# Both exponentials of a unit's first step placed ahead of the next unit's copies of logits in ScalarE's order

## The chip, the cores and the metric

The kernel runs on one core of a Trainium2 chip. The core has a matrix engine (TensorE, PE in the profile), a vector engine (VectorE, DVE), an activation engine (ScalarE, ACT), GpSimd (POOL) and SyncE (SP), which here only issues DMAs. Each engine works through its own instructions in the order in which the program lists them, and waits at an instruction until the semaphores that it names have come. The metric is the device time of one execution in microseconds (us); less is better. Before the change it is 3184.22 us, the median of three runs (3184.0 to 3186.14).

## What is computed

Eight images of 512 channels and 32 x 32 pixels pass two layers in float32. The first layer normalizes over groups, and applies a block with two bottlenecks, each of which holds a 3 x 3 convolution and an attention over all 1024 pixels with 4 heads of 64 channels; the second normalizes again and applies a grouped 1 x 1 convolution whose groups come from tables. What matters here is the attention:

```python
qkv = conv2d(x, qkv_w, 0).reshape(b, 3, HEADS, HD, hw)
q, k, v = (qkv[:, 0], qkv[:, 1], qkv[:, 2])
r = (rw + rh).reshape(1, HEADS, HD, hw)
logits = jnp.einsum('bhdi,bhdj->bhij', q, k + r) * HD ** (-0.5)
a = jax.nn.softmax(logits, axis=-1)
out = jnp.einsum('bhij,bhdj->bhdi', a, v)
...
z = jax.nn.silu(bn_eval(conv2d(z, m_cv2_w[i], 0), m_cv2_bn[i]))
ys.append(yi + z)
```

Around it stand `t = cbs(x, cv1_w, ...)`, `z = cbs(yi, m_cv1_w[i], ..., 1)` and `cbs(concatenate(ys), cv2_w, ...)`, where `cbs` is a convolution, a scale and shift per channel, and SiLU.

## The kernel before

**Units.** The attention is cut into 64 units, counted here from 0. A unit is one image, one of the two bottlenecks, one pair of heads (`hp`) and one half of the queries (512 of them). Its keys come in 8 chunks `t` of 128 (`KT = 8`). The logits of a chunk are held with the keys on the partitions and 512 queries of each of the two heads along the row, as a tile `st` of 128 x 1024 in SBUF.

**What a unit issues** (class `Unit`):

- `logits(t)`: TensorE multiplies a chunk of keys with the queries into two PSUM banks `lg`, one for each head (L511); ScalarE copies each bank to `st` (L518); from the second chunk on VectorE takes the running maximum `mx` over the chunks (L523), reading the bank as well.
- `top()` and `spread()`: TensorE transposes `mx`, VectorE reduces it to the negated maximum of each query (`nm`, L532), and TensorE spreads that over the partitions (`mb`, L540).
- `soften(t)`: VectorE adds `mb` to `st` (L545). `exponent(t)`: ScalarE takes the exponential of `st` in place (L549), and from the second chunk on GpSimd adds it to the sum `acc` in four pieces (L556).
- `values(t)`: TensorE multiplies the exponentials with `v` and accumulates over all eight chunks in one bank `po` (L563). There is one such bank for all units (`ps_o`, one buffer).
- `finish()`: TensorE sums `acc` over the partitions into a bank `den` (L577), and ScalarE copies that to `rb` (L580). `divide(part)`: VectorE takes the reciprocal of `rb` (L584) and multiplies `po` with it into `q` (L586), a half at a time. Only then may the next unit's first `values` write `po`.

**The loop.** Units overlap: while unit `u` takes exponentials and multiplies with `v`, the logits of the next unit `nxt` are computed. A unit has four steps, `t` = 0, 2, 4 and 6, with two chunks each. In the first step the unit before it (`before`) is also brought to its end: its `finish`, its last two `values` and its `divide`.

**Background work.** All other matrix work (the 1 x 1 and 3 x 3 convolutions, `q`, `k`, `v`, and so on) is kept in generators. After each step `advance` takes as much of it as a share of a counted time says, so that TensorE has work between a step's chain of softmax operations and the next. `clock.tick` moves the counted time on, and operations that are set for a due time (the normalization of loaded tiles, L165, for one) are issued when it has passed. Background results are read by ScalarE as SiLU (L130) or copies, and by VectorE.

**Banks.** `lg`, `den`, the transposed maxima and all background results share five PSUM banks (`ps_f`). The ten `st` buffers (`stp`) hold the eight chunks of a unit and the first two of the next.

**What sets the order.** A scheduler places the instructions of each engine before the program runs. Where its choice isn't wanted the order is written out by hand: `pe_turn`, `act_turn` and `in_turn` tie each instruction that is passed to them to the one passed before it on the same engine (TensorE, ScalarE, VectorE). For ScalarE only two kinds are tied so: the copies of logits, and the exponentials:

```python
act_turn(nc.scalar.copy(st[:, h], lg[h]))        # logits, L518
act_turn(nc.scalar.activation(st, st, AF.Exp))   # exponent, L549
```

The copy of `den` to `rb`, the SiLUs, the normalizations and the other copies are not tied. ScalarE loads a table (ACT_TABLE_LOAD in the profile) when it goes from SiLU to the exponential, and again when it goes back; plain copies need none.

In steps 2, 4 and 6 ScalarE's tied order is `exponent(t)`, four copies, `exponent(t + 1)`. In step 0 it is four copies, `exponent(0)`, `exponent(1)`.

Of the kernel before, what the change touches and what calls it, by code (L numbers as in the profile page):

```python
# [39 lines left out]
def conv_preact_kernel(ctx: ExitStack, tc: tile.TileContext, x, cv1, cv2, mcv1, qkv, mcv2, bn, rw, rh, conv, s_in, t_in, out):  # L40
# [868 lines left out]
    def slot_filler(s):  # L909

        prev = slots[s - 1] if s else (None, 0)
        nxt = slots[s + 1] if s + 1 < len(slots) else (None, 0)
        todo, needed = [], 0.0

        def add(us, g):
            nonlocal needed
            todo.append((us, g))
            needed += us

        im, i = nxt  # L920
        add(8.0, bg.take(8.0))
        if im and i == 1:
            add(7.0, im.conv_m2(0))
            add(0.0, call(im.transform, 1, 3.0, 1.0))
            add(9.0, bg.take(9.0))
        products = im.conv3(i) if im else iter(())
        if prev[1] == 1:
            if im:
                add(21.3, (us for _, us in zip(range(16), products)))
            add(7.0, prev[0].conv_m2(1))  # L930
            add(0.0, call(lambda: finishing(prev[0])))
        if im:
            add(10.7 if prev[1] == 1 else 32.0, products)
            add(7.0, bg.take(7.0))
        if im:
            add(21.0, im.project(i))
        if s + 2 < len(slots) and slots[s + 2][1] == 0:
            add(0.0, call(slots[s + 2][0].load_y))
            add(0.0, call(slots[s + 2][0].transform, 0, 8.0, 1.3))
        rest = SHARE - needed if im else 70.0  # L940
        if rest > 0:
            todo.append((rest, bg.take(rest, wait=True)))
        total = sum(c for c, _ in todo)
        return needed, total, todo
# [77 lines left out]
    for s in range(len(slots)):  # L1022
        needed, total, todo = slot_filler(s)
        state = {"done": 0.0}

        def filler():
            for us, g in todo:
                start = state["done"]
                for cost in g:
                    clock.tick(cost)  # L1030
                    state["done"] += cost
                    yield

                state["done"] = max(state["done"], start + us)

        fill = filler()

        def advance(share):
            goal = max(share * total, min(1.0, share / 0.74) * needed + 0.1)
            while state["done"] < goal:  # L1040
                if next(fill, "end") == "end":
                    break

        steps = 4 * (KT + 2)
        for j in range(4):
            u = units[4 * s + j]
            nxt = units[4 * s + j + 1] if 4 * s + j + 1 < len(units) else None
            base = j * (KT + 2)

            advance((base + 0.7) / steps)  # L1050
            u.top()
            clock.tick(0.9)
            advance((base + 1.4) / steps)
            u.spread()
            clock.tick(0.9)
            advance((base + 2) / steps)
            for t in range(0, KT, 2):
                if before and t == 0:
                    before.finish()
                    clock.tick(0.9)  # L1060
                u.soften(t)
                u.soften(t + 1)
                if t:
                    u.exponent(t)

                lag = u if t else before
                if lag:
                    lag.values((t - 2) % KT)
                    lag.values((t - 1) % KT)
                    clock.tick(2.0)  # L1070
                if before and t == 0:
                    before.divide(0)
                    before.divide(1)
                if nxt:
                    nxt.logits(t)
                    nxt.logits(t + 1)
                    clock.tick(2.0)

                if not t:
                    u.exponent(t)  # L1080
                u.exponent(t + 1)
                advance((base + 4 + t) / steps)
            before = u
        for _ in fill:
            pass
# [62 lines left out]
```

## Time and profile before

| | |
|---|---|
| time of three runs, median (lowest to highest) | 3184.22 us (3184.0 to 3186.14) |
| the profiled execution's own time | 3188.51 us |
| its span, first to last instruction | 3186.8 us |
| mean granted clock of TensorE | 0.993 |
| busy: TensorE matmuls / VectorE / ScalarE / GpSimd | 3085.9 / 2050.6 / 1717.3 / 1395.3 us |
| 512 exponentials (L549) | 539.1 us, 1068 ns each |
| 1024 copies of logits (L518) | 524.4 us, 596 ns each |
| 2048 matmul records of `values` (L563) | 500.3 us; TensorE idle just before them 21.7 us |

The profile is of one execution. A group's row gives its busy time, the mean of one instruction, and the time for which its engine stood idle just before it, with what ended that idle time. A float32 matmul shows as two records, and the two heads' matmuls of `logits`, `values` and `finish` run side by side, so their records overlap. Matmul ends are modelled, and successive ones overlap; what counts is the time from start to start. In a timeline the columns are start, length, engine, line, operation, what is written and read, and, in brackets, the idle time of the engine before it with its releaser. "PEclk" is the granted clock of TensorE as a share of full speed.

### The profile page before, as it was taken

Reading aid. Unit: us, or ns where it says so; the run is one execution under the profiler, and the core shown is the slowest. Engines: PE = TensorE matmul, PEld = TensorE weight load, DVE = VectorE, ACT = ScalarE, POOL = GpSimd, SP = SyncE. Lnnn points to the kernel's source line nnn. Section 1 sums busy time; section 2 is a strip of 40 time slices with the busy share of each in tenths; the row PEclk is TensorE's granted clock in tenths of the full one; section 3 lists DMA queues with packets and bytes.
Section 4 is the critical chain, followed back from the end, with each engine's and each line's share of the span. In section 5 each row is a group of like instructions: output and inputs, shape, how many; then the busy total and the mean of one; then the engine's idle time right before and its main releaser. Section 6 shows DMA issues by size and latency. Waiting matters only on the chain.

```text
span 3186.8 us, 34171 instructions
## 1 busy us (share of the span) xinstructions
PE 3085.9 (97%) x11668; PEld 1522.9 (48%) x11668; DVE 2050.6 (64%) x2718; ACT 1717.3 (54%) x2347; POOL 1395.3 (44%) x1867
## 2 busy tenths in 40 slices
PE   7999999999999999999999999999999999999999
PEld 3645444454445454454445454454445454453333
DVE  5446576667666676667666676667766676666742
ACT  3255765854655555544656455554656455555631
POOL 2114444446444454445444454355434454455420
PEclk9999999999999999999999999999999999999999
DMA  8851442421233232424233332424233332413366
GB/s 294 287 187 63 154 161 83 149 79 65 88 109 129 93 119 70 148 86 137 89 109 129 119 114 75 139 83 142 90 113 132 110 122 71 145 63 129 110 212 216
DMA packets 142014, 399.35 MB, mean 125 GB/s; under 512 B 13072, under 2 KB 14352, under 8 KB 141840
## 3 DMA queue, kind: packets, MB, share of 16 engines
q1 hardware_dynamic: 141120, 396.94, 36.4%
q8 instruction: 92, 1.51, 0.2%
q14 instruction: 82, 0.67, 0.1%
q10 hardware_dynamic: 720, 0.23, 0.0%
HBM read 317.42 MB, written 79.69 MB: 125 GB/s over the span
## 4 chain that ended last, share of the span: by engine, by line
PE 70%; DVE 7%; ACT 5%; issue 3%; DMA 2%; POOL 1%; ACTq 0%; DVEq 0%; SPq 0%; POOLq 0%
PE m L313 14%; PE cv L175 12%; PE lg L511 11%; PE po L563 11%; PE qk L175 6%; PE l L175 6%; PE v L405 3%; PE m L175 2%; DVE st L545 2%; PE mb L540 2%; ACT st L518 2%; PE mt L531 2%; PE den L577 2%; DVE mx L523 1%; ACT st L549 1%
## 5 line engine op out<-in xcount | busy, mean ns | idle before, releaser
L556 POOL TENSOR_TENSOR sum<-sum,st 128x256 f32<-128x256 f32 x1536 | 1126.1, 767 | 570.1 <-ACT st L549 565.0
L523 DVE TENSOR_TENSOR mx<-mx,lg 128x512 f32<-128x512 f32 x768 | 477.8, 681 | 412.2 <-ACT st L518 412.2
L549 ACT ACTIVATE st<-st 128x1024 f32<-128x1024 f32 x512 | 539.1, 1068 | 340.2 <-DVE st L545 338.8
L518 ACT COPY st<-lg 128x512 f32<-128x512 f32 x1024 | 524.4, 596 | 351.7 <-PE lg L511 306.6
L545 DVE TENSOR_TENSOR st<-st,mb 128x1024 f32<-128x1024 f32 x512 | 603.7, 1213 | 63.6 <-PE mb L540 63.6
L313 PE MATMUL m<-plane,w_m 128*128 128x256 f32 x2304 | 537.4, 388 | 21.8 <-DVE x2r L487 9.0
L556 POOL TENSOR_TENSOR sum<-st,st 128x256 f32<-128x256 f32 x256 | 188.0, 766 | 789.4 <-ACT st L549 789.3
L563 PE MATMUL po<-st,v 128*64 128x512 f32 x2048 | 500.3, 608 | 21.7 <-ACT st L549 14.7
L511 PE MATMUL lg<-q,k 64*128 64x512 f32 x2048 | 513.7, 619 | 1.6 <-ACT y L130 1.5
L313 PEld LDWEIGHTS m<-plane,w_m 128*128 128x128 f32 x2304 | 433.0, 192 | 149.0 <-issue 44.1
L175 PE MATMUL cv<-y,w_cv 128*128 128x512 f32 x1024 | 465.4, 599 | 10.8 <-DVE mx L523 6.2
L511 PEld LDWEIGHTS lg<-q,k 64*128 64x128 f32 x2048 | 178.6, 187 | 330.1 <-issue 266.4
L175 PEld LDWEIGHTS cv<-y,w_cv 128*128 128x128 f32 x1024 | 185.7, 190 | 251.7 <-issue 227.8
L563 PEld LDWEIGHTS po<-st,v 128*64 128x64 f32 x2048 | 128.9, 137 | 327.5 <-issue 228.9
L175 PE MATMUL l<-x,w_l 128*128 128x512 f32 x512 | 235.8, 603 | 10.3 <-DVE mx L523 10.0
L175 PE MATMUL cv<-x,w_cv 128*128 128x512 f32 x512 | 233.4, 603 | 8.5 <-ACT x L165 2.4
L175 PE MATMUL qk<-z,w_qkv 128*128 128x512 f32 x512 | 234.0, 600 | 1.7 <-DVE mx L523 1.7
L584 DVE RECIPROCAL rb<-rb 128x256 f32<-128x256 f32 x128 | 215.4, 1723 | 30.6 <-ACT rb L580 30.5
L532 DVE TENSOR_REDUCE nm<-mt 128x4 f32<-128x512 f32 x128 | 82.4, 685 | 158.6 <-PE mt L531 158.5
L580 ACT COPY rb<-den 128x512 f32<-128x512 f32 x64 | 37.3, 583 | 226.9 <-PE den L577 226.9
L175 PEld LDWEIGHTS l<-x,w_l 128*128 128x128 f32 x512 | 92.7, 190 | 132.3 <-issue 107.2
L175 PEld LDWEIGHTS cv<-x,w_cv 128*128 128x128 f32 x512 | 94.3, 192 | 126.4 <-issue 107.3
(145 smaller groups left out, 2404.3 us busy)
## 6 DMA issues: line engine op xcount, KB each, us to landing
w_m<-w_m SPq DMA_DIRECT2D x96, 768.0 KB, 4.8
w_cv<-in_cv SPq DMA_DIRECT2D x90, 512.0 KB, 3.5
y<-y SPq DMA_DIRECT2D x64, 512.0 KB, 4.4
x<-in_x SPq DMA_DIRECT2D x56, 512.0 KB, 5.4
y<-y SPq DMA_DIRECT2D x64, 256.0 KB, 3.5
k<-r SPq DMA_DIRECT2D x32, 512.0 KB, 3.6
res<-y SPq DMA_DIRECT2D x32, 512.0 KB, 4.0
xr<-in_x SPq DMA_DIRECT2D x32, 512.0 KB, 4.0
```

The source lines that it names most:

```text
L175: nc.tensor.matmul(ps, w, moving, start=(n == 0), stop=(n == len(terms) - 1))
L313: nc.tensor.matmul(ps[:, ts(co, 256)].rearrange("p (t x) -> p t x", x=F), w[:, co, c, dx], u[:, 9 * c : 9 * c + 8, dx : dx + F], start=(j ...
L405: nc.tensor.matmul(ps[:, ts(j, P)], z[:, c, ts(4 * j4 + j, P)], w[:, c, 512 + P * hp : 512 + P * hp + P], start=(c == 0), stop=(c == IT - 1),)
L511: nc.tensor.matmul(lg[h], self.k[r, ts(t, P)], self.q[r, self.hp, ts(self.half, HALF)], start=True, stop=True)
L518: act_turn(nc.scalar.copy(st[:, h], lg[h]))
L523: in_turn(nc.vector.tensor_tensor(self.mx[:, h], so_far[:, h], lg[h], ALU.max))
L532: nc.vector.tensor_reduce(self.nm[:, h], mt, AX.X, ALU.max, negate=True)
L545: in_turn(nc.vector.tensor_tensor(st, st, flat(self.mb), ALU.add))
L549: act_turn(nc.scalar.activation(st, st, AF.Exp))
L556: nc.gpsimd.tensor_tensor(flat(self.acc)[:, part], flat(so_far)[:, part], st[:, part], ALU.add)
L563: nc.tensor.matmul(self.po[HD * h : HD * h + HD], self.v[:, t, ts(h, HD)], self.st[t][:, h], start=(t == 0), stop=(t == KT - 1),)
L584: nc.vector.reciprocal(self.rb[:, r], self.rb[:, r])
```

## The change

In step 0 both exponentials now stand right after the two `soften`, as in the other steps the first of the two does; so they come ahead of `before.values`, `before.divide` and `nxt.logits` in the program, and ahead of the four copies of logits in ScalarE's tied order. Steps 2, 4 and 6 are as they were. No instruction is added or removed, and no tile or DMA is changed; the counted time of the background work is ticked as before. `exponent(0)` issues one exponential; `exponent(1)` issues one exponential and GpSimd's first four additions to `acc`, which move with it.

```diff
                 u.soften(t)
                 u.soften(t + 1)
-                if t:
-                    u.exponent(t)
+                u.exponent(t)
+                if not t:
+
+                    u.exponent(1)
 
                 lag = u if t else before
                 if lag:
...
                     nxt.logits(t + 1)
                     clock.tick(2.0)
 
-                if not t:
-                    u.exponent(t)
-                u.exponent(t + 1)
+                if t:
+                    u.exponent(t + 1)
                 advance((base + 4 + t) / steps)
```

## The prediction

> **What bounds the kernel now.** First the page: TensorE's busy time, and the chain that ended last.
>
> ```profile
> span 3186.8 us, 34171 instructions
> ...
> PE 3085.9 (97%) x11668; PEld 1522.9 (48%) x11668; DVE 2050.6 (64%) x2718; ACT 1717.3 (54%) x2347; POOL 1395.3 (44%) x1867
> ...
> PE 70%; DVE 7%; ACT 5%; issue 3%; DMA 2%; POOL 1%; ACTq 0%; DVEq 0%; SPq 0%; POOLq 0%
> ```
>
> TensorE works or is about to for 97% of the span; only some 100 us of idle time can be won. The groups of instructions say how much of it the exponentials own:
>
> ```profile
> L563 PE MATMUL po<-st,v 128*64 128x512 f32 x2048 | 500.3, 608 | 21.7 <-ACT st L549 14.7 <-DVE mx L523 6.9
> ```
>
> TensorE stands idle 21.7 us in all before `values`. Next the timelines of step 0. ScalarE in unit 30, which loads a table:
>
> ```profile
> 1557.83 0.58 ACT L580 COPY rb<-den 128x512 f32<-128x512 f32 x1 [5.45 <-PE den L577]
> 1560.64 2.05 ACT L518 COPY st<-lg 128x512 f32<-128x512 f32 x4 [2.23 <-PE lg L511]
> 1562.71 1.28 ACT L549 ACT_TABLE_LOAD   x1
> 1564.00 2.00 ACT L549 ACTIVATE st<-st 128x1024 f32<-128x1024 f32 x2
> ```
>
> ScalarE idles 2.23 us after `rb`, waiting for logits, though the softened tiles lie ready; 2.2 us appears in almost every unit, because `den`, two `values` and two `logits` always take TensorE that long. 37 of the 64 units have the load before `exponent(0)`, 27 don't. Unit 27 is one that does not, and TensorE waits in it (PE, ACT and DVE timelines):
>
> ```profile
> 1441.07 2.02 PE L563 MATMUL po<-st,v 128*64 128x512 f32 x8 [1.23 <-DVE mx L523]
> ...
> 1435.22 0.58 ACT L580 COPY rb<-den 128x512 f32<-128x512 f32 x1 [4.79 <-PE den L577]
> 1438.01 2.05 ACT L518 COPY st<-lg 128x512 f32<-128x512 f32 x4 [2.20 <-PE lg L511]
> 1439.92 2.04 ACT L549 ACTIVATE st<-st 128x1024 f32<-128x1024 f32 x2
> ...
> 1434.25 2.35 DVE L545 TENSOR_TENSOR st<-st,mb 128x1024 f32<-128x1024 f32 x2 [0.95 <-PE mb L540]
> 1436.52 3.36 DVE L584 RECIPROCAL rb<-rb 128x256 f32<-128x256 f32 x2
> 1439.79 0.69 DVE L586 TENSOR_TENSOR q<-po,rb 128x256 f32<-128x256 f32 x2
> ```
>
> The named releaser is doubtful: `values(0)` starts 0.05 us after `exponent(0)` ends (1439.92 + about 1.1), so that is what it waited for. But the last reader of `po`, the multiply of `divide`, ends at 1440.48, 0.59 us before. That is the next wait behind the one removed.
>
> Last, the stretches around unit 60, whose stall is the longest (3.72 us by the PE timeline):
>
> ```profile
> 2916.74:2920.15 3.41, 2.48 (x6) 0.73 (x8) 2.35 (x3) 2.77 (x3) 1.51 (x3) 0.50 0.00 0
> 2920.15:2923.57 3.42, 3.42 (x10) 1.18 (x8) 0.00 (x0) 0.11 (x1) 3.42 (x6) 0.50 0.00 0
> ```
>
> The granted clock (third from the end) is 0.50 in two stretches of 3.4 us after it.
>
> [...]
>
> **The change part by part.** No instruction is added; ScalarE's order in step 0 becomes `rb`, (load), two exponentials, four copies.
>
> *The exponentials, earlier.* Without a load they take 0.96 + 1.06 = 2.0 us and fit the 2.2 us of idle time: the copies do not move. With a load, 0.58 + 1.29 + 2.0 = 3.9 us from the start of `rb` against 2.8 before: the copies leave 1.05 us later. Where `soften(1)` ends late (eight units, up to 2.5 us after `rb` starts) the sum is nearly the same. Either way ScalarE's step ends about 2 us earlier, since the idle time is used.
>
> *What the exponentials are worth.* I took each place where TensorE's start-to-start time exceeds the usual before the first `values(0)`: 17 units, 19.4 us together. In eleven (7, 11, 12, 23, 27, 28, 39, 43, 44, 55, 59; 0.5 to 2.5 us each) `po` was freed only 0.58 to 0.61 us before the start, so at most 0.43 to 0.55 is won: 5.4 us. In units 16, 32 and 48 (0.65 each) `po` is free 2.2 us before; 3 x 0.55 = 1.65. Unit 19: 1.45 less the 0.1 that any wait costs, 1.35. Unit 60: 3.89 with `po` free 2.03 before: 1.97. Unit 62: 0.16. Sum 10.5 us. Where `po` stays the wait, what is late next is `divide`, two reciprocals of 1.7 us behind `soften(1)` on VectorE.
>
> *Clock.* The stalls of units 60 and 11 fall from 3.9 to 1.9 and from 2.45 to 1.9 us. The matmuls after them lost 0.90 + 0.99 + 1.01 + 0.31 = 3.2 us and about 1.6 us to the half clock; I take that as won. It could be nothing or be lost elsewhere[...].
>
> *ScalarE's head start.* In unit 8 ScalarE is without a pause from 588.8 to 610 us and TensorE waits 2.30 us for the SiLU of a bank at 610.2; 2 us earlier, that gives 2.0. In units 24, 40 and 56 a wait of 0.76 for a maximum that follows late copies goes: 2.0. Together 4; bounded by 0 and 5.
>
> *The copies, later.* Behind them wait: background matmuls for banks, the maximum `mx`, and through it `soften(2)`. After the four `logits` the next bank in line is mostly that of `den` or older. The first bank freed by these copies is wanted 1.5 to 1.9 us after the copy ended in the tightest ordinary units, more in the rest, so 1.05 us is covered; without this cover it would cost up to 1.05 x 36 = 38 us. Four units have less: unit 0 (0.13), 3 (0.36), 4 (0.05), and 7 (1.08, no load, not delayed). In unit 3 the copies started with `logits`, only 0.43 us after `rb`, so they leave 2.8 late: 2.5 lost. In unit 4 normalizations (L165) wait for a load between `rb` and copies: with the exponentials ahead 1.5 lost, behind them 3.3. Unit 0: 2.0, of which the next exponential wait (1.40 at 236.4) takes back about half. Together 5 us, between 2 and 10. The maximum starts up to 1 us later; then `soften(2)` too, but `exponent(2)` behind SiLU and two loads has time (1569.41 in unit 30): 0.
>
> *GpSimd.* Its first four additions start 2 us earlier; it idles before them (14 us in unit 29), and copies that wait for it (45.0 us in 23 waits) come off sooner: nothing on the path. No DMA is issued by what moved, and none is passed in the SP or GpSimd queue.
>
> Sum: -10.5 - 4.8 - 4 + 5 = -14.3. Later waits on VectorE's maxima (2.0 us at 1457.9 in unit 27, say) run partly by themselves and take some back; I keep four fifths of it, -12. Against the profiled execution: 3188.5 - 12 = 3176.5. Its time lies 4.3 above the median, so in runs 3184.2 - 12 = 3172.
>
> **Rivals.**
>
> 1. *Given back:* the stall moves to `po` and to the later bank waits. For: the eleven places with 0.6 us. Against: most waits follow TensorE's own work and move with it. Gain 2 to 5 us: 3181.
> 2. *Slower: copies starve the banks.* Only the tied instructions have a written order; the scheduler may put a SiLU between the exponentials or ahead of the copies. One costs two loads or at least 1.28 + 0.78 us on top of 1.05, so the copies leave 3.1 late and pass the point of 1.9 us from which banks decide: 1.2 us in perhaps 25 units, 30 us, less the 12: 3202. For: units 19, 35 and 51 already have four normalizations among the copies. Against: SiLUs of earlier work stand ahead of `rb`, and their data come before.
> 3. *No effect* can't be: the tied order is the program's. But `exponent(0)` could go ahead of `rb`, which isn't tied; then `divide` is late by up to 0.5 us in the eleven units, the 5.4 falls away, and the end is 3177.
>
> **How the numbers follow.** A measurement of this kernel tells 0.2% (6.4 us) from no change. The main case, with rival 3 in it, 0.62: 3172, its own range 3164 to 3178. Given back 0.22: 3178 to 3186. Slower 0.16: 3190 to 3215. So faster 0.62, same 0.22, slower 0.16; the range 3162 to 3187 leaves out the slower case and a little below.
>
> **What would show it.** Right: ScalarE's timeline reads `rb`, load, exponentials, copies, with the 2.2 us gone; idle time before `values` falls from 21.7 to about 11, now ended by VectorE's multiply; unit 60's clock stays at 1; TensorE idles 1 to 3 us more in units 0, 3 and 4 only. Wrong: more table loads than the 222 of before, or new idle time of background matmuls ended by copies L518 in many units; or a scheduler that, seeing the exponentials earlier, shuffles background matmuls of the same step, which no row of before can show.

## The result, and the profile after

| | before | after |
|---|---|---|
| median (lowest to highest) | 3184.84 us (3183.04 to 3190.34, 6 runs) | 3202.7 us (3201.55 to 3208.15, 6 runs) |
| span of the profiled execution | 3186.8 us | 3199.8 us |
| table loads on ScalarE | 222 | 262 |

The ratio is 1.0058 with a 95% interval of 1.0045 to 1.0071: slower by about 18 us, where 12 us less was forecast. The page of the kernel after has the engines' busy time and the chain that ended last:

```profile
span 3199.8 us, 34204 instructions
...
PE 3095.4 (97%) x11668; PEld 1529.7 (48%) x11668; DVE 2038.1 (64%) x2718; ACT 1772.5 (55%) x2387; POOL 1390.3 (43%) x1867
...
PE 73%; DVE 5%; ACT 5%; issue 2%; DMA 2%; POOL 0%; ACTq 0%; DVEq 0%; SPq 0%; POOLq 0%
```

TensorE still sets the end. It does the same 11668 records and is busy 9.5 us longer, at a mean granted clock of 0.991 instead of 0.993; ScalarE has 40 instructions more. The groups of the kernel after say what these are, and what became of the wait of `values`:

```profile
L563 PE MATMUL po<-st,v 128*64 128x512 f32 x2048 | 496.0, 602 | 17.2 <-DVE q L586 8.9 <-ACT st L549 6.2 <-ACT st L518 2.1
...
L130 ACT ACT_TABLE_LOAD x131 | 168.1, 1283 | 14.9 <-PE m L175 7.1
L549 ACT ACT_TABLE_LOAD x130 | 166.8, 1283 | 2.3
```

The 40 are table loads, 20 on each side, of 1283 ns each. The last of the 262 stands at L657, and none at a copy. Idle time before `values` fell from 21.7 to 17.2 us, and VectorE's multiply of `divide` is now its largest releaser, at 8.9 us. Unit 27 shows that as it was foreseen (PE timeline, kernel after):

```profile
1457.99 1.94 PE L563 MATMUL po<-st,v 128*64 128x512 f32 x8 [0.79 <-DVE q L586]
```

and its ScalarE timeline:

```profile
1452.59 0.58 ACT L580 COPY rb<-den 128x512 f32<-128x512 f32 x1 [4.79 <-PE den L577]
1453.07 2.00 ACT L549 ACTIVATE st<-st 128x1024 f32<-128x1024 f32 x2
1455.38 2.05 ACT L518 COPY st<-lg 128x512 f32<-128x512 f32 x4 [0.30 <-PE lg L511]
```

The 2.20 us of idle time before the copies became 0.30, the two exponentials stand in it, and `values(0)` waits for `po`. Unit 60 is as foreseen too (PE timeline, kernel after): the stall is 1.84 us instead of 3.72, and the matmuls behind it run at full clock (the granted clock is 1.00 from 2933.70 to 2950.00 us).

```profile
2933.72 1.94 PE L563 MATMUL po<-st,v 128*64 128x512 f32 x8 [1.84 <-ACT st L518]
2935.58 1.99 PE L511 MATMUL lg<-q,k 64*128 64x512 f32 x8
```

The copy that is named as releaser here isn't read by `values`. What they waited for is `po`: they start 0.15 us after the last multiply of `divide` ended (2933.57), as those of unit 27 start 0.14 us after theirs, and in run 10 below the same 1.84 us are put down to that multiply.

**Where the time came from.** I took the start of each unit's first `mb` transposition from both traces, and between two of them split the time into TensorE's records and the gaps. Differences, after less before, in us (units 0 to 4 sum to +21.1):

| units | gaps | records | sum |
|---|---|---|---|
| 0 | +1.8 | +1.5 | +3.4 |
| 1 and 2 | +0.9 | +1.2 | +2.1 |
| 3 and 4 | +9.9 | +5.6 | +15.5 |
| 5 to 62 | -9.6 | +0.1 | -9.5 |
| 63 and the end | -0.4 | 0.0 | -0.3 |

Longer records are not the clock alone: the mean granted clock of unit 0 is 1.00 in both traces. In units 3 and 4 TensorE ran at half clock for 13.7 us instead of 3.4. At half clock the records of 128x512 at L175 start 853 ns after one another, at full clock 429 ns (medians of 17 and 2484 in the kernel after), so I take half of the time at half clock as lost: an estimate of up to 5.1 us. The gain is there, spread over the units from 5 on (some 6 of the 9.5 us may belong to this one trace of the kernel before; see the last section); five units at the start lose more than twice as much. The view of stretches, one for unit 3 and one for unit 4, of the kernel before (length, then busy time of PE, PEld, DVE, ACT and POOL, granted clock, DMA share, GB/s):

```profile
349.65:396.72 47.07, 47.07 (x153) 19.36 (x152) 27.65 (x42) 39.24 (x50) 20.46 (x29) 1.00 0.46 158
396.72:449.38 52.66, 47.87 (x169) 22.54 (x168) 36.49 (x51) 38.89 (x50) 24.66 (x30) 0.97 0.60 205
```

and of the kernel after:

```profile
356.92:412.51 55.59, 49.55 (x154) 19.88 (x152) 27.42 (x42) 43.71 (x53) 20.46 (x29) 0.97 0.38 130
412.51:472.28 59.77, 51.10 (x169) 24.28 (x170) 36.12 (x51) 45.56 (x55) 24.69 (x30) 0.91 0.52 179
```

Here ScalarE was busy for 39.24 of 47.07 us (83%) and 38.89 of 52.66 (74%) before the change, against 54% over the span. It has three and five instructions more after it, and TensorE's clock falls to 0.97 and 0.91. A high share alone isn't what hurts, though. In units 7 and 8 ScalarE was busy for 88% and 84% in the kernel before (fourth engine in each line), and the change cost them nothing (-0.4 and +0.1 us):

```profile
542.15:582.21 40.06, 38.95 (x135) 15.84 (x134) 24.55 (x35) 35.44 (x44) 20.45 (x29) 1.00 0.24 77
582.21:629.92 47.71, 44.24 (x159) 20.26 (x158) 32.04 (x40) 40.24 (x50) 21.04 (x28) 1.00 0.54 177
```

Unit 3 on ScalarE, before:

```profile
353.30 1.52 ACT L165 ACTIVATE x<-x,go_a,gr_a 128x512 f32<-128x512 f32 x2 [1.14 <-DVE gms_a L148]
354.73 0.76 ACT L130 ACTIVATE y<-cv,bn_b,bn_s 128x512 f32<-128x512 f32 x1
355.39 0.57 ACT L580 COPY rb<-den 128x512 f32<-128x512 f32 x1
356.39 2.05 ACT L518 COPY st<-lg 128x512 f32<-128x512 f32 x4 [0.43 <-PE lg L511]
358.46 1.28 ACT L549 ACT_TABLE_LOAD   x1
```

and after:

```profile
358.63 1.52 ACT L165 ACTIVATE x<-x,go_a,gr_a 128x512 f32<-128x512 f32 x2 [0.61 <-DMA y<-y]
360.16 1.28 ACT L549 ACT_TABLE_LOAD   x1
361.46 1.06 ACT L549 ACTIVATE st<-st 128x1024 f32<-128x1024 f32 x1
362.53 1.28 ACT L130 ACT_TABLE_LOAD   x1
363.83 0.78 ACT L130 ACTIVATE y<-cv,bn_b,bn_s 128x512 f32<-128x512 f32 x1
364.50 0.57 ACT L580 COPY rb<-den 128x512 f32<-128x512 f32 x1
365.10 1.28 ACT L549 ACT_TABLE_LOAD   x1
366.39 1.06 ACT L549 ACTIVATE st<-st 128x1024 f32<-128x1024 f32 x1
367.35 2.03 ACT L518 COPY st<-lg 128x512 f32<-128x512 f32 x4
```

The scheduler put `exponent(0)` with its load, and a second load to go back, between the normalizations and the SiLU. That SiLU empties the bank that the next logits need. From the start of the second normalizations the SiLU comes 5.20 us later instead of 1.43, and the copies 8.72 instead of 3.09. TensorE's waits in unit 3 and then unit 4, from the PE timeline after:

```profile
364.66 1.12 PE L511 MATMUL lg<-q,k 64*128 64x512 f32 x2 [0.23 <-ACT y L130]
...
367.97 5.42 PE L175 MATMUL cv<-x,w_cv 128*128 128x512 f32 x12 [1.88 <-ACT st L518]
...
388.83 7.11 PE L175 MATMUL cv<-x,w_cv 128*128 128x512 f32 x12 [2.52 <-ACT y L130]
...
422.63 1.12 PE L511 MATMUL lg<-q,k 64*128 64x512 f32 x2 [2.39 <-ACT y L130]
...
427.35 5.01 PE L175 MATMUL m<-q,w_m 128*128 128x512 f32 x7 [2.25 <-ACT st L518]
```

Banks are emptied late by SiLUs and by copies, and twelve matmuls take 7.11 us where as many took 5.42 earlier in the unit: half clock (the granted clock is 0.50 from 389.92 to 393.33 us). With a wait of 1.41 us for the negated maximum `nm`, at 412.51, the waits of unit 3 are all of its 6.0 us of gaps.

Unit 4 had long waits before the change, too (PE timeline, kernel before):

```profile
408.37 6.88 PE L175 MATMUL m<-q,w_m 128*128 128x512 f32 x12 [2.84 <-ACT st L518]
...
440.70 5.45 PE L313 MATMUL m<-plane,w_m 128*128 128x256 f32 x24 [1.49 <-DVE mx L523]
```

Its waits in step 0 grew from 3.3 to 5.4 us, and the later ones for the running maximum `mx` from 1.5 to 3.2 us.

In the whole program ScalarE's order in step 0 is `rb`, exponentials in 27 units only (unit 0 has no `rb`). In 36 `exponent(0)` stands ahead of `rb`, and in ten of these (3, 4, 6, 8, 16, 24, 32, 40, 48 and 56) a SiLU stands between the two exponentials, with a load on each side of it.

### The profile page after: what moved, and what is told of

The parts are those of the page before. It is cut to its first block, busy times and chain, and to the rows that moved or that the text cites. A ratio compares the mean times of both kernels' runs of the same rounds, so it can differ in the third digit from the quotient of the medians.

```text
span 3199.8 us, 34204 instructions
## 1 busy us (share of the span) xinstructions
PE 3095.4 (97%) x11668; PEld 1529.7 (48%) x11668; DVE 2038.1 (64%) x2718; ACT 1772.5 (55%) x2387; POOL 1390.3 (43%) x1867
## 4 chain that ended last, share of the span: by engine, by line
PE 73%; DVE 5%; ACT 5%; issue 2%; DMA 2%; POOL 0%; ACTq 0%; DVEq 0%; SPq 0%; POOLq 0%
PE cv L175 14%; PE m L313 14%; PE lg L511 11%; PE po L563 11%; PE qk L175 6%; PE l L175 6%; PE v L405 3%; PE m L175 2%; PE mb L540 2%; PE mt L531 2%; PE den L577 2%; DVE st L545 1%; ACT st L549 1%; ACT st L518 1%; DVE mx L523 1%
## 5 line engine op out<-in xcount | busy, mean ns | idle before, releaser
L563 PE MATMUL po<-st,v 128*64 128x512 f32 x2048 | 496.0, 602 | 17.2 <-DVE q L586 8.9
L175 PE MATMUL cv<-y,w_cv 128*128 128x512 f32 x1024 | 464.1, 598 | 2.1 <-DMA y<-y 1.1
L556 POOL TENSOR_TENSOR sum<-st,st 128x256 f32<-128x256 f32 x256 | 177.9, 727 | 657.7 <-ACT st L549 640.9
L175 PEld LDWEIGHTS cv<-y,w_cv 128*128 128x128 f32 x1024 | 186.0, 190 | 240.8 <-issue 229.9
L175 PE MATMUL cv<-x,w_cv 128*128 128x512 f32 x512 | 237.9, 612 | 14.2 <-ACT y L130 4.4
L175 PE MATMUL l<-x,w_l 128*128 128x512 f32 x512 | 238.5, 608 | 10.2 <-DVE mx L523 7.6
L175 PE MATMUL qk<-z,w_qkv 128*128 128x512 f32 x512 | 234.0, 600 | 1.1 <-DVE mx L523 1.1
L130 ACT ACT_TABLE_LOAD x131 | 168.1, 1283 | 14.9 <-PE m L175 7.1
L549 ACT ACT_TABLE_LOAD x130 | 166.8, 1283 | 2.3
L175 PEld LDWEIGHTS cv<-x,w_cv 128*128 128x128 f32 x512 | 95.9, 195 | 135.3 <-issue 110.3
```

What stands on the lines that cost most here:

```text
L130: nc.scalar.activation(dst, src, AF.Silu, bias=bn_b[:, col : col + 1], scale=bn_s[:, col : col + 1])
L175: nc.tensor.matmul(ps, w, moving, start=(n == 0), stop=(n == len(terms) - 1))
L556: nc.gpsimd.tensor_tensor(flat(self.acc)[:, part], flat(so_far)[:, part], st[:, part], ALU.add)
L563: nc.tensor.matmul(self.po[HD * h : HD * h + HD], self.v[:, t, ts(h, HD)], self.st[t][:, h], start=(t == 0), stop=(t == KT - 1),)
```

## The experiments

Times are medians, and ratios are to runs of the kernel before made in the same session on the same chip (whose medians were 3187.16 us for the first four, 3186.42 for the next four and 3190.41 for the last two). Letters name the theories of one expectation only. "Units 3 and 4" below means the time from the start of unit 3 to that of unit 5, less that of the kernel before, from the traces.

**1. `rb` tied ahead of the exponentials.** The kernel after with one tie more:

```diff
-            nc.scalar.copy(self.rb, den)
+            act_turn(nc.scalar.copy(self.rb, den))
```

> The change, with the copy of den to rb put into ScalarE's tied order, so that no exponential of step 0 can stand ahead of it or of the SiLU before it. The program then has 246 table loads (262 after the change, 222 before). Theory A (the loss is exponential 0 slipping ahead of rb and of a SiLU, with two more loads each time): most of the 18 us goes, 3178 to 3190. Theory B (the exponentials ahead of the copies are the loss, the copies starve the banks in whatever order rb stands): 3198 to 3206.

3202.16 us, ratio 1.0047 (1.0029 to 1.0065), 246 loads. The splits are gone, the order is that of the prediction, and units 3 and 4 still lose 12.3 us. Their PE timeline:

```profile
362.10 7.11 PE L175 MATMUL cv<-x,w_cv 128*128 128x512 f32 x12 [2.26 <-ACT st L518]
...
384.86 5.42 PE L175 MATMUL cv<-x,w_cv 128*128 128x512 f32 x12 [2.73 <-ACT y L130]
```

Now the first SiLU and `rb` are on time, and the load and the exponentials sit ahead of the copies instead. So the place of `exponent(0)` against `rb` isn't the main cause: 12.3 of the 15.5 us stay. Even in this order the program has 24 loads more than before the change. This run's one trace has a further 7.2 us after the start of unit 63, and they are of another kind: VectorE's operation L150, of 128x4 elements, took 8.96 us there (0.16 in the kernel before) and ended with GpSimd's additions, and TensorE waited 5.96 us for what follows it. So the time of this run says less about the order than units 3 and 4 do.

**2 and 3. The change in the units from 5 on, and in units 0 to 4 alone** (run 3 has `< 5` in place of `>= 5`).

```diff
-                u.exponent(t)
-                if not t:
-                    u.exponent(1)
+                ahead = 4 * s + j >= 5
+                if t or ahead:
+                    u.exponent(t)
+                if ahead and not t:
+                    u.exponent(1)
...
-                if t:
+                if not t and not ahead:
+                    u.exponent(t)
+                if t or not ahead:
                     u.exponent(t + 1)
```

> The change in units 5 to 63 only; units 0 to 4 have the order of before. Theory A, with the loss in units 0, 3 and 4 (21 us there by the offset of the units in the two profiles): 3176 to 3184, at or below before. Theory B or any cost spread over the units: 3195 to 3203.

3181.49 us, ratio 0.998 (0.9969 to 0.999).

> The change in units 0 to 4 only. Theory A with the loss in units 0, 3 and 4: 3201 to 3212, more than the whole change. A cost spread over the units: 3185 to 3188.

3209.43 us, ratio 1.0065 (1.0051 to 1.0079). The two parts, about -6 and +21 us by their ratios, each known to 3 to 5 us, add up to about 14 of the 18. The loss sits in five units, and the rest of the change is a small gain.

**4. The change from unit 5 on, with `rb` tied** (the edits of 1 and 2 together).

> The change in units 5 to 63 with rb tied ahead: the order that the prediction had assumed, without the units with little slack. Theory A and the prediction's sum for these units (10.5 + 4.8 + 4, four fifths kept): 3168 to 3178. Given back at later waits: 3179 to 3186. Theory B: above 3190.

3187.72 us, ratio 0.9996 (0.9984 to 1.0007). With `rb` kept first no gain is left that can be told from none, where 3168 to 3178 us was expected; the intervals of runs 2 and 4 still touch. The gaps of units 5 to 62 are 4.4 us less than before, against 8.9 in run 2. The scheduler's freedom to put `exponent(0)` first, which rival 3 counted as a loss, seems to be a help there.

**5. The late copies taken off ScalarE.** The kernel after; in units 0, 3 and 4 VectorE makes the copies of step 0:

```diff
-                act_turn(nc.scalar.copy(st[:, h], lg[h]))
+                if by_vector:
+                    in_turn(nc.vector.tensor_copy(st[:, h], lg[h]))
+                else:
+                    act_turn(nc.scalar.copy(st[:, h], lg[h]))
...
+                    by_vector = t == 0 and 4 * s + j in (0, 3, 4)
```

> The changed kernel, but in units 0, 3 and 4 the four copies of logits of step 0 are made by VectorE, tied into its order ahead of the maximum, instead of ScalarE behind the exponentials. Theory A (the loss of units 0 to 4 is the lateness of these copies: banks stay full, TensorE waits, and the new stalls bring half clock): TensorE's waits ended by copies L518 go in units 3 and 4; idle and half clock of units 0 to 4 come from +21 us against the kernel before to +6 or less; time 3182 to 3190. Theory B (ScalarE is full of SiLUs and table loads in units 3 and 4, and it is these that are late, wherever the copies stand): at least +12 us stay in units 0 to 4, with waits ended by SiLU L130; time 3195 to 3203. Theory C (VectorE becomes the late one): new waits ended by maxima or the division, time 3190 to 3205.

3192.96 us, ratio 1.0024 (1.0015 to 1.0032). Units 0 to 4 lose 13.7 us, 12.1 of it in units 3 and 4. That is what theory B expected (at least 12); the time lies between the ranges of A and B, and within that of C (3190 to 3205). Half of A is right, since the waits for the copies are gone. Of C there is little: in unit 4 TensorE waits 1.26 and 2.83 us for maxima, but the second wait stands in the kernel after as well. In unit 3 this is left (PE timeline):

```profile
360.78 1.50 PE L511 MATMUL lg<-q,k 64*128 64x512 f32 x2 [1.73 <-ACT y L130]
...
362.66 8.16 PE L175 MATMUL cv<-x,w_cv 128*128 128x512 f32 x12
```

The logits wait for the SiLU behind `exponent(0)`, as in the kernel after. After the wait of 1.73 us the granted clock is 0.50 (stretches below), and twelve matmuls take 8.16 us instead of 5.42. In units 3 and 4 of this run the gaps grew by 4.3 us and the records by 7.9.

The length of a wait doesn't decide this alone, since in run 1 the clock is 1.00 after one of 2.73 us. In each trace the stretches at half clock begin at multiples of 3.413 us from one another (the 11 of the kernel before and the 14 of the kernel after to within 0.03 us), and what shows a connection is the time without a matmul between two marks of this grid. In run 5 one interval holds all of the 1.73 us; in run 1 the mark at 383.00 splits the 2.73 us into 0.87 and 1.86 (stretches of run 5, then of run 1):

```profile
357.99:361.40 3.41, 1.68 (x6) 0.48 (x3) 1.45 (x3) 3.36 (x5) 0.00 (x0) 1.00 0.00 0
361.40:364.81 3.41, 3.41 (x7) 1.57 (x6) 3.41 (x4) 2.16 (x2) 1.16 (x2) 0.50 0.21 77
...
383.00:386.41 3.41, 1.55 (x4) 0.84 (x5) 1.10 (x2) 3.40 (x6) 2.62 (x4) 1.00 0.25 93
386.41:389.83 3.42, 3.42 (x10) 1.36 (x8) 3.42 (x5) 3.39 (x4) 0.58 (x1) 1.00 0.00 0
```

In the twelve traces, from 100 us on, 81 intervals at full clock have 2.2 us or more without a matmul, and half clock follows every one of them; it follows 36 of the 95 with 1.67 to 2.2 us, and none with less. The kernels before and after alone have 15 of 15, 6 of 14, and none of 1325. These are counts in the traces of this kernel and its variants; what sets the clock they don't show. Against the start of the span the grids of these two traces lie 0.96 us apart, so the same wait need not be split alike in two executions.

**6 and 7. The kernel before and the kernel after without table loads.** SiLU becomes the identity in both; its nonlinearity is left out, so that one load is left in the program.

```diff
-        nc.scalar.activation(dst, src, AF.Silu, bias=..., scale=...)
+        nc.scalar.activation(dst, src, AF.Identity, bias=..., scale=...)
```

> The kernel before with SiLU replaced by the identity everywhere (the nonlinearity is left out), so that only one table load remains in the program. It is the base of the next run. 222 loads of 1.28 us go, 284 us of ScalarE's time. All theories: faster than the kernel before by 10 to 45 us, since waits for SiLUs and late ScalarE work go.

3183.73 us, ratio 0.9989 (0.9983 to 0.9996). A miss: 284 us less work on ScalarE gave 3 us, not 10 to 45.

> The changed kernel with SiLU replaced by the identity everywhere (the nonlinearity is left out), one table load. Against the same edit of the kernel before: theory A1 (the order alone makes the copies late enough): units 0 to 4 still lose 10 us or more. Theory A2 (it is the table load between the copies and their place, which the changed order puts ahead of them): without loads the exponentials fit the 2.2 us of idle time, and units 0 to 4 lose 4 us or less. In units 5 to 63 both expect a gain of 4 to 10 us less idle time, and a time 0 to 10 us below that of the kernel before with the same edit under A2, 0 to 12 us above it under A1.

3182.96 us, ratio 0.9985 (0.9976 to 0.9995). Without loads the changed order costs nothing overall. Against run 6, units 0 to 4 lose 3.9 us, all of it in the records (their gaps differ by -0.1), and units 3 and 4 together 1.7 (run 6 itself is 4.1 us longer there than the kernel before). Theory A2 holds, if only just: it allowed 4 us. From unit 5 on the idle time is 3.8 us less than in run 6, where 4 to 10 were expected. Unit 3 on ScalarE in run 7:

```profile
355.23 1.04 ACT L549 ACTIVATE st<-st 128x1024 f32<-128x1024 f32 x1
356.17 0.76 ACT L130 ACTIVATE y<-cv,bn_b,bn_s 128x512 f32<-128x512 f32 x1
356.83 0.57 ACT L580 COPY rb<-den 128x512 f32<-128x512 f32 x1
357.30 1.06 ACT L549 ACTIVATE st<-st 128x1024 f32<-128x1024 f32 x1
358.26 2.04 ACT L518 COPY st<-lg 128x512 f32<-128x512 f32 x4
```

The order is that of the kernel after, SiLU between the exponentials and all, but from `exponent(0)` to the copies it takes 3.03 us instead of 5.89, and TensorE's first wait in unit 3 is 0.46 us. So it is not the order alone that hurts in units 3 and 4, but the order with table loads in it.

**8. The change in unit 3 alone** (`ahead = 4 * s + j == 3`).

> The kernel before with the changed order in unit 3 alone. If unit 4 loses on its own account: from the start of unit 3 to that of unit 4 +7 to +11 us against the kernel before, and from unit 4 to unit 5 within 2 us of nothing; end +7 to +12, time about 3196. If unit 4's loss is unit 3's handed on through late normalizations and loads of x: +4 us or more also from unit 4 to unit 5, end +12 to +19, time 3201. If unit 3's loss itself was handed on from unit 0: under +4 from unit 3 to unit 4, time within 0.2% of before.

3196.27 us, ratio 1.0029 (1.0018 to 1.004). From unit 3 to 4 the trace has +9.0 us, and from unit 4 to 5 +0.4. Unit 3 loses on its own account, and neither its loss nor late loads of `x` are handed on; unit 4's +7.0 us in the kernel after go with the change in unit 4 itself, which I did not run alone. In the kernel after the loads of `x` do start later against the unit's start, and a store of `y` ahead of them in SP's queue waits for the late SiLU. But the store was issued at 364.63 us and the load at 369.99, when TensorE's matmuls released its buffer: a consequence of the stall.

**9. Both cures: copies by VectorE, and `rb` tied, in units 0, 3 and 4.** The edit of 5, and

```diff
-            nc.scalar.copy(self.rb, den)
+            rb = nc.scalar.copy(self.rb, den)
+            if tied:
+                act_turn(rb)
...
-                    before.finish()
+                    before.finish(4 * s + j in (0, 3, 4))
```

> As e5_vec_copies (the changed kernel, in units 0, 3 and 4 the four copies of step 0 by VectorE), and in those units the copy rb is tied into ScalarE's order ahead of the exponentials, which keeps the SiLU of the background convolution and rb ahead of exponent 0 and its table load. Theory D (the loss of units 3 and 4 is a chain on ScalarE: one table load and two exponentials are put ahead of something whose bank TensorE wants within 2 us; of the SiLU and rb where exponent 0 goes ahead of them, as in the changed kernel, of the copies where rb is tied, as in e1_rb_first): with both out of the way units 3 and 4 lose 4 us or less together, against 15.5 in the changed kernel, 12.3 in e1_rb_first and 12.1 in e5_vec_copies; no wait of logits for SiLU L130 is left in units 3 and 4; time 3178 to 3187. Rival E (ScalarE or VectorE has simply too much to do in these units): 8 us or more stay, time 3188 to 3196.

3192.09 us, ratio 1.0000 (0.9993 to 1.0008). The loss of the change is gone, but the time lies in the range of rival E (3188 to 3196) and not in that of theory D (3178 to 3187); the kernel before, measured beside it, took 3190.41 us, 3 to 6 us more than in the other comparisons. Unit 3 behaves as theory D says: +1.8 us, where the kernel after has +8.5 and run 5 +6.4. Unit 4 doesn't: +5.9. From the PE timeline, unit 3 and then unit 4:

```profile
361.39 5.42 PE L175 MATMUL cv<-x,w_cv 128*128 128x512 f32 x12
...
412.32 1.94 PE L566 MATMUL po<-st,v 128*64 128x512 f32 x2 [3.12 <-DVE q L591]
414.19 6.13 PE L175 MATMUL m<-q,w_m 128*128 128x512 f32 x12
...
438.28 1.98 PE L175 MATMUL cv<-x,w_cv 128*128 128x512 f32 x4 [1.24 <-DVE mx L526]
...
448.79 7.13 PE L313 MATMUL m<-plane,w_m 128*128 128x256 f32 x24 [2.83 <-DVE mx L526]
```

No logits wait for a SiLU any more, and in unit 3 the twelve matmuls run at full clock. In unit 4 the scheduler, which has the exponentials earlier, puts the first `values` ahead of twelve background matmuls (the other order stands in the kernel before), and they wait 3.12 us for `divide`. But in the kernel before TensorE waits about as long at this place, 2.84 us for the copies. What unit 4 has on top comes later: it waits 1.24 and 2.83 us for maxima, against 1.49 before. That is 2.6 of the 2.8 us by which its gaps grew; the records grew by 3.1. The kernel after and runs 1 and 5 have such waits too (3.2, 4.2 and 4.1 us in unit 4), and so has run 7 without loads (3.1, and 2.1 in run 6). So D is shown for unit 3. For unit 4 it isn't, and rival E, too much work for ScalarE or VectorE, isn't excluded there; what makes these maxima late stays open. Units 3 and 4 sum to 7.7 us: more than D's 4, and just under the 8 of E.

**10. `exponent(0)` alone ahead, from unit 5 on.** As run 2, with `exponent(1)` left behind the copies:

```diff
-                if ahead and not t:
-                    u.exponent(1)
...
-                if t or not ahead:
-                    u.exponent(t + 1)
+                u.exponent(t + 1)
```

> From unit 5 on exponent 0 alone goes ahead of the copies; exponent 1 stays behind them. Units 0 to 4 as in the kernel before. If the gain is that values 0 no longer waits for exponent 0 (the prediction's step), half the change has all of it: as e2_from5, 3178 to 3185, and unit 60 still gains 4 us. If the earlier end of the whole step on ScalarE matters (the head start for SiLUs and later steps), it gains less: 3184 to 3190.

3181.93 us, ratio 0.9968 (0.9956 to 0.998). By the times, half of the change has all of its gain (run 2: 0.998, and the intervals overlap). By the traces it has less: the gaps of units 5 to 62 fall by 5.7 us, not 8.9, and the rest of what this trace gains there, 7.4 us, is in the records. Unit 60 gains 4.4 us (4.3 in run 2). The group of `values` in this run:

```profile
L563 PE MATMUL po<-st,v 128*64 128x512 f32 x2048 | 496.0, 603 | 16.8 <-DVE q L586 10.8 <-ACT st L549 5.8 <-ACT st L518 0.2
```

This version is faster than the kernel before by about 0.3% (0.2 to 0.4); it was not measured side by side with the kernel after.

## Why the prediction was wrong

*The exponentials, earlier: failed.* The step took ScalarE's order to be "`rb`, (load), two exponentials, four copies" in all units, with the SiLUs ahead of `rb`. That order stands in 27 of 64. Only tied instructions keep their order; the exponentials, no longer tied behind copies that wait for logits, were free to pass `rb` and SiLUs, and did in 36 units. The step put new table loads at none, and the program has 40 more: `rb` tied takes away 16 of them, and the other 24 come even with the order that the step assumed (run 1). The text named the passing in rivals 2 and 3, gave rival 2 a chance of 0.16, and held against it that "SiLUs of earlier work stand ahead of `rb`". In units 3 and 4 that was true in the kernel before because the copies held the exponentials back.

*The copies, later: failed, and it decides the sign.* The step had the three places right (units 0, 3 and 4) and the price wrong: 5 us, between 2 and 10. Measured were 3.4 us in unit 0 and 15.5 in units 3 and 4. Four things were left out:

- Half clock after new stalls. The clock was counted as a gain where stalls go, and never as a cost where they come; in units 3 and 4 by the estimate above it is up to 5.1 of the 15.5 us. It followed a wait of 1.73 us in run 5 and one of 2.52 us in the kernel after, both shorter than the 3.72 us of unit 60.
- The SiLU as a second victim. The step followed banks freed by copies, but not the bank freed by a SiLU that now stands behind `exponent(0)`. At unit 3's first place run 5 shows it alone (1.73 us) and run 1 the copies alone (2.26 us); in either run units 3 and 4 lose 12 us.
- A second stall in unit 3 (2.52 us at 388.83). The bank needed is again that of a SiLU, on a ScalarE that is busy for 27.2 of the 30 us from 360 to 390.
- The maxima. The step put what follows from them at 0; in unit 4 the waits for `mx` grew by 1.7 us, and in runs 1, 5 and 9 by 2.6 to 2.7.

For unit 3's first place the size was right where the order was the assumed one: 2.5 us foreseen, and 2.26 in run 1. That the kernel after has 0.23 + 1.88 us there is luck, as its copies come 5.63 us later than before and not 2.8. In unit 0 a part of the loss is another thing that the text had put among what "would show it wrong": the scheduler put a first `values` ahead of background matmuls, where it waits 1.39 us.

*What the exponentials are worth: right in kind, too large.* `po` is the next wait, as the text said; it ends about half of what is left before `values` (8.9 of 17.2 us, where about 11 us were foreseen in all), and the exponentials still end 6.2 us. The 0.1 us that the step lets any wait cost was an estimate: in the trace of the kernel before TensorE starts 0.04 to 0.11 us after the end of the ScalarE instruction that is named as its releaser (the middle nine tenths of 325 waits over 0.1 us). In units 7, 23, 39, 55 and 59 the step of the offset between both traces is -0.4 to -0.6 us, in 16, 32 and 48 -0.6 each, in 60 -4.3. But unit 19 lost 1.5 where 1.35 was to be won, 28 and 44 (+0.3 each) won nothing, and 27 and 43 lost 1.7 each to the clock. A gain that the text didn't have stands against it: 1.7 us each in units 15, 31 and 47, whose gaps went.

*Clock: won where said, lost elsewhere.* The step's 4.8 us were an estimate from the matmuls behind two stalls. Units 60 and 11 gain 4.3 and 2.9 us, stall and clock together, where 5.2 and 2.1 were forecast; 1.1 us of unit 60's stands in runs 3 and 8 too, which have the old order there. In the sum over units 5 to 62 TensorE ran at half clock for 34.0 us instead of 37.4, worth 1.7 us by the same halving and not 4.8, and its records take 0.1 us more; the text had named that bound ("lost elsewhere").

*ScalarE's head start: smaller.* In unit 8 the gaps fall by 1.4 us (2.0 foreseen), and half clock takes the same amount back. In units 24, 40 and 56 the wait for a maximum is gone as foreseen, and they bring 2.8 us together by this trace (2.0 foreseen). That the sum fits is not shown to be the change's doing: runs 3 and 8, with the old order there, have 2.0 and 2.2 us less, too.

*GpSimd and DMA: held.* Run 8 and the release of the loads of `x` show no transfer that became the cause in units 3 and 4.

*The sum.* Four fifths of 14.3 us are 11.4, not 12; that is small beside the rest. The gains were 19.3 us before the fifth was taken off, and run 2 has about 6; the loss was 5 us, and run 3 has about 21.

*The rivals.* Rival 2 gave the measured time (3202) and the right ingredient, two loads around a SiLU between the exponentials, but another place: small losses in 25 units, instead of large ones in two. None of the other eight split units loses more than 0.1 us against the kernel before, so that the time fits is luck. Rival 3's premise happened, and run 4 speaks against its sign.

What stays open: what lengthened the records of unit 0 by 1.5 us at full clock, and why the maxima of unit 4 are late. Unit 2 lost 2.1 us in the kernel after, and about as much in run 9, but nothing in runs 1, 3 and 5, which share its order or nearly so: only those two have a stretch of half clock in it (at 348.96 and 343.97 us).

## What to carry to other kernels

Before an instruction is moved ahead on an engine, ask in each stage what then comes later, and how soon another engine wants it. The engine's busy share doesn't tell: the move cost 15.5 us in two units in which ScalarE was 83% and 74% busy, and nothing in two at 88% and 84%. In unit 3 TensorE wanted a bank 0.36 us after the copy that freed it, by the prediction's reading, and another that a SiLU had to empty. A tie that is moved also frees what it held back, so ask which untied instruction the scheduler can now pass, and what a table load on the way (1.28 us here) costs the one that is passed. Count half clock as a risk of each stall that a change makes, as for each that it takes away (in units 3 and 4 it rose from 3.4 to 13.7 us), and apply a change of order only in the stages in which it gains.

## What the runs showed that I had not expected

- 221 of the 222 table loads, 284 us of ScalarE's time, are worth only 3 us in the kernel before (run 6), yet the presence of loads decides whether the change costs anything: with them its ratio is 1.0058, and without them 0.9985 against 0.9989 for the unchanged order.
- Half clock can cost more than the wait ahead of it: in unit 3 of run 5 a wait of 1.73 us is followed by 6.83 us at half clock, worth up to 3.4 us if half of that is lost.
- One trace has an uncertainty of its own. In runs 3 and 8 each engine has the instructions of units 5 to 62 in the order of the kernel before, and these units took 5.9 and 6.2 us less, 3.1 of it in unit 36 at the clock. So of the -9.5 us in the table above some 6 may belong to the trace of the kernel before, and the gain from unit 5 on is better read from run 2's ratio. Units 3 and 4 vary as well: with the old order they are 1.1 to 1.4 us longer in runs 2, 4 and 10 than in the trace of the kernel before, and run 3, with the order of the kernel after in them, loses 19.3 us there, not 15.5. The gaps are steadier: 9.9 us in the kernel after and 10.9 in run 3, against 8.5 in run 1, 4.3 in run 5 and 3.7 in run 9.
